# Routing logits of a fused two-layer block: routing weights as the stationary operand, in four column blocks, with one transpose back per group

## The chip, the cores and the metric

The kernel runs on one core of a Trainium2 chip. The metric is device time in microseconds (us) of one execution; the time before is the median of three runs. Engines are named as the profile does: PE is TensorE's matmul side and PEld its weight loads, DVE is VectorE, ACT is ScalarE, POOL is GpSimd, SP is SyncE.

## The reference

Two layers, each a gated attention-like step and a gated feed-forward step, on 32 sequences of 128 tokens with 128 features. All parts run in the kernel; the change touches the last one.

```python
x = x + tanh(g_xattn[0]) * L0_xattn(layernorm(x), ctx, ctx, ...)   # mLSTM, 8 heads
x = x + tanh(g_ffn[0])   * L0_ffn(layernorm(x), W1, b1, W2, b2)    # quantized, 128 -> 512 -> 128
x = x + tanh(g_xattn[1]) * L1_xattn(ctx, layernorm(x))             # dynamic time warping, then a gather-add
x = x + tanh(g_ffn[1])   * L1_ffn(layernorm(x), gate_weight, w1, b1, w2, b2)

def L1_ffn(x, gate_weight, w1, b1, w2, b2):
    logits = einsum('bld,ed->ble', x, gate_weight)          # 8 experts
    kth_val = sort(logits.reshape(-1))[4 * 128 * 6 - 1]     # over all sequences
    gates = logits * (logits >= kth_val)
    h = gelu(einsum('bld,ehd->bleh', x, w1) + b1)           # 128 -> 512
    y = einsum('bleh,edh->blde', h, w2) + b2.T              # 512 -> 128
    return einsum('blde,ble->bld', y, gates)
```

The routing logits are the product of the normed tokens with an 8 x 128 matrix. One threshold over all 32 x 128 x 8 logits decides which of them weigh an expert's output and which count as zero.

## The kernel before, in words

**Stages.** X, the residual, stays in SBUF with tokens on partitions: [128 tokens, 32 sequences, 128 features]. Four sequences make a group, so there are eight groups. The first layer runs up to about 229 us of the profiled execution. Then the warp (the second layer's alignment) is done twice by `warp_steps`, first for groups 0 to 2, alone on VectorE, then for groups 3 to 7. A row of it is a minimum (line 1058) and a scan (line 1059) on VectorE; `meet` (line 1003) and the turn-round at the end (lines 1098 and 1109) are small products. While the first warp runs, `second_dense` (lines 1241 to 1289) does the rest of the first layer's feed-forward on ScalarE, PE and GpSimd (line 1251 is GpSimd's add), and writes distances to DRAM (line 1236; for the first groups line 1156).

**The expert loop** starts at about 370 us. It has 64 units, one for a group and an expert. A unit has four products of 128 x 512 into `mph` (line 1494), each followed by a GELU on ScalarE into `hT` (line 1499), and sixteen products of 128 x 128 into `mpo` (line 1507). All are float32, and an fp32 product shows as two records on PE. The first 24 units are those of groups 0 to 2. Of the first 34 units (HELD) the output is copied (line 1515) and sent to DRAM, since its weight GA isn't known yet; from unit 34 on `combine` (lines 1457 and 1462) adds outputs to X on VectorE, the held ones read back among them. The program asks for GA there.

**The background.** Beside the units runs a generator, `background()`: `aligned(1)`, `aligned(2)`, the second warp, `aligned(3)` to `aligned(7)`, then `search()`. `pump(0.85)` after each mph, and after each four mpo, draws steps from it until the planned times that they yield add up. So a yield's number moves all later steps against the units. `aligned(0)` comes before the loop. Tile's scheduler then fixes the order of instructions on each engine at build time, and every engine keeps to its own order.

**One group's `aligned(g)`** (lines 1316 to 1364): masks `ge` and `pt` on VectorE (lines 1325 and 1327) and four products into `px` (line 1328) gather the aligned context; the residual add (line 1332) and the norm follow on VectorE, ending in `y` (line 1348); four transposes (line 1351) and a ScalarE copy give YT (line 1353), features on partitions. Then the routing logits: four products (line 1357), each with one sequence's 128 x 128 block of YT as the stationary operand and the routing weights `gws` (8 columns) as the moving one, give tokens on partitions and 8 columns for a sequence. VectorE copies these 32 columns into `lg` (line 1360).

**The search** (lines 1376 to 1401) finds the threshold bit by bit in 31 steps: VectorE counts (line 1371), PE sums over partitions (line 1373), VectorE decides (lines 1393 and 1394). It needs `lg` of all groups.

The PSUM pool `p_k` has a single buffer with the tag `small`, which the logits, the warp's small products and the search's sums share. In the first stage lines 453 and 614 write products with 32 stationary columns into blocks of 32 PSUM partitions; line 215 is the transposes of the first norm.

Of the kernel before, what the change touches and what calls it, by code (L numbers as in the profile page):

```python
# [8 lines left out]
F32 = mybir.dt.float32  # L9
# [9 lines left out]
P = 128  # L19
# [7 lines left out]
E = 8  # L27
KTH = 4 * 128 * 6
GB = 4
NG = B // GB  # L30
HW = 32
# [12 lines left out]
def tile_flamingo_gated(  # L44
# [21 lines left out]
    nc = tc.nc  # L66

    def pool(stack, name, bufs=1, space=None, side=None):
        kw = {} if space is None else {"space": space}
        kw.update({} if side is None else {"side": side})  # L70
        return stack.enter_context(tc.tile_pool(name=name, bufs=bufs, **kw))

    def new(p, shape, dt, tag, bufs=None):
        kw = {} if bufs is None else {"bufs": bufs}
        return p.tile(shape, dt, tag=tag, name=tag, **kw)
# [19 lines left out]
    gws = new(keep, [P, E], F32, "gws")  # L95
# [26 lines left out]
    ident = new(keep, [P, P], F32, "ident")  # L122
# [27 lines left out]
    def row_norm_steps(p, v, n, mean, r):  # L150

        m, w = (8, "") if n <= 8 else (16, "_w")
        bn = new(p, [P, m, 6], F32, "bn" + w)[:, 0:n]
        for i in range(n):
            nc.vector.bn_stats(bn[:, i, :], v[:, i, :])
            if i % 2 == 1:
                yield

        df = new(p, [P, m], F32, "bn_df" + w)[:, 0:n]
        nc.vector.tensor_tensor(df, bn[:, :, 1], bn[:, :, 4], ALU.subtract)  # L160
        ve = new(p, [P, m], F32, "bn_ve" + w)[:, 0:n]
        nc.vector.scalar_tensor_tensor(
            ve, bn[:, :, 2], D * 1e-5, bn[:, :, 5], ALU.add, ALU.add
        )
        nc.vector.scalar_tensor_tensor(mean, df, -0.5, bn[:, :, 1], ALU.mult, ALU.add)
        yield
        nc.vector.scalar_tensor_tensor(df, df, 0.25, df, ALU.mult, ALU.mult)
        nc.vector.scalar_tensor_tensor(ve, ve, 1.0 / D, df, ALU.mult, ALU.add)
        yield
        for _ in root_steps(p, ve, n, r):  # L170
            yield
# [116 lines left out]
    YT = new(wide, [P, B, S], F32, "YT")  # L288
    xst = new(wide, [P, 2, NG], F32, "xst")
    with ExitStack() as st:  # L290
        ap = pool(st, "attn")
        gp = pool(st, "gates")
        lp = pool(st, "ln", bufs=2)
# [105 lines left out]
        for k in range(6):  # L399
# [3 lines left out]
                rhs=one_c[0:1, :], start=True, stop=True,  # L403
# [6 lines left out]
        for k in range(2):  # L410
            hr_ps = new(p_at, [P, 4, S], F32, "at")
            nc.tensor.matmul(
                hr_ps, lhsT=sel.rearrange("p j c h -> p (j c h)"),
                rhs=ind[:, 4 * k : 4 * k + 4, :], start=True, stop=True,
# [303 lines left out]
        for p in range(B // 2 + 1):  # L718
# [4 lines left out]
            for u in range(3):  # L723
# [6 lines left out]
                g = p // 2 + 1  # L730
# [67 lines left out]
    with ExitStack() as st:  # L798
# [18 lines left out]
        with ExitStack() as st2:  # L817
# [26 lines left out]
            for n in range(4):  # L844
                for c in range(NC):
                    ph = new(p_h, [P, 2, 512], F32, "ph")
                    for k in range(2):
# [3 lines left out]
                            start=True, stop=True,  # L851
# [91 lines left out]
    def idle(busy, tie, value, n):  # L943

        if value is not None:
            rows = value.shape[0]
            one = onesb if value.dtype == BF16 else ones
            tie = nc.tensor.matmul(
                busy[:, 0 : value.shape[1]], lhsT=one[0:rows, :], rhs=value, start=True, stop=True
            )  # L950
        for _ in range(n):
            with tc.issue_after(getattr(tie, "ins", tie)):
                tie = nc.tensor.matmul(busy, lhsT=onesb, rhs=w1q, start=True, stop=True)  # L953
# [164 lines left out]
    with ExitStack() as st:  # L1118
        dp = pool(st, "dist", bufs=2)
        lp = pool(st, "lnA", bufs=2)  # L1120
# [16 lines left out]
        for g, ym2, ysq in normed:  # L1137
            d2 = new(dps, [P, GB, S], F32, "d2")
            nc.tensor.matmul(d2, lhsT=ones, rhs=ysq, start=True, stop=False)  # L1139
            for i in range(GB):  # L1140
                nc.tensor.matmul(
                    d2[:, i, :], lhsT=CD[:, GB * g + i, :], rhs=ym2[:, i, :],
                    start=False, stop=(i == GB - 1),
                )
            dd = new(dp, [P, GB, S], F32, "dd")
            for i in range(GB):
                b = GB * g + i
# [152 lines left out]
    with ExitStack() as st:  # L1300
        mp = pool(st, "moe")
        lp = pool(st, "last", bufs=2)
# [4 lines left out]
        p_k = pool(st, "p_k", space=PSUM)  # L1307
# [4 lines left out]
        lg = new(mp, [P, B * E], F32, "lg")  # L1312
        z = new(mp, [P, B * E], F32, "z")
        junk = new(mp, [P, B * E], BF16, "junk")

        def aligned(g):

            grp = slice(GB * g, GB * g + GB)
            xb = X[:, grp, :]
            px = new(p_x, [P, GB, D], F32, "px")  # L1320
            for i in range(GB):
                b = GB * g + i
                way = ends[0][:, :, b : b + 1] if b < BP else ends[1][:, :, b - BP : b - BP + 1]
                ge = new(lp, [P, S], BF16, "ge")
                nc.vector.tensor_scalar(ge, jota, way[:, 0], None, ALU.is_ge)
                pt = new(lp, [P, S], F32, "pt", bufs=4)
                nc.vector.scalar_tensor_tensor(pt, jota, way[:, 1], ge, ALU.is_le, ALU.mult)
                got = nc.tensor.matmul(  # L1328
                    px[:, i, :], lhsT=pt, rhs=CT[:, b, :], start=True, stop=True
                )  # L1330
                yield 0.65
            nc.vector.scalar_tensor_tensor(xb, px, tgx[:, 1:2], xb, ALU.mult, ALU.add)
            if g == 0:

                busy = new(p_k, [P, HID], F32, "small")
                idle(busy, got, None, 2)
                idle(busy, None, xb[:, 0, 0:4], 3)
            yield 0.8
            mean = new(lp, [P, 8], F32, "bn_mean")[:, 0:GB]
            r = new(lp, [P, 8], F32, "bn_r")[:, 0:GB]  # L1340
            for _ in row_norm_steps(lp, xb, GB, mean, r):
                yield 0.5
            if g == 0:
                idle(busy, None, mean, 6)
            tp = new(p_x, [P, GB, S], F32, "px")
            for i in range(GB):
                y = new(lp, [P, D], F32, "y", bufs=4)
                got = nc.vector.tensor_scalar(
                    y, xb[:, i, :], mean[:, i : i + 1], r[:, i : i + 1], ALU.subtract, ALU.mult
                )  # L1350
                nc.tensor.transpose(tp[:, i, :], y, ident)  # L1351
            held["normed"] = getattr(got, "ins", got)
            nc.scalar.copy(YT[:, grp, :], tp)
            yield 1.2
            lg_ps = new(p_k, [P, GB, E], F32, "small")
            for i in range(GB):
                nc.tensor.matmul(  # L1357
                    lg_ps[:, i, :], lhsT=YT[:, GB * g + i, :], rhs=gws, start=True, stop=True
                )
            got = nc.vector.tensor_copy(  # L1360
                lg[:, E * GB * g : E * GB * (g + 1)], lg_ps.rearrange("p b e -> p (b e)")
            )
            held["aligned", g] = getattr(got, "ins", got)
            yield 0.2
# [38 lines left out]
        def second_part():  # L1403

            with ExitStack() as st2:
                wp = pool(st2, "warpB", bufs=2, side="right")
                w1p = pool(st2, "warpB1", side="right")
                DV = CD[0 : 2 * (B - BP)].rearrange("p b s -> p (b s)").bitcast(BF16).rearrange(
                    "p (r s) -> p r s", s=S
                )  # L1410
                for w in warp_steps(
                    BP, B - BP, wp, w1p, lambda shape, tag: new(p_k, shape, F32, "small"),
                    nc.sync, DV, ends[1], masks[1],
                ):
                    yield w
            for g in range(NP, NG):
                for w in aligned(g):
                    yield w
            for w in search():
                yield w  # L1420

        def background():
            for g in range(1, NP):
                for w in aligned(g):
                    yield w
            for w in second_part():
                yield w
# [50 lines left out]
        for _ in aligned(0):  # L1478
            pass
# [6 lines left out]
        for n, (k, p, g, j) in enumerate(units):  # L1486
            e = 2 * p + j
# [4 lines left out]
            for c in range(NC):  # L1492
                ph = new(p_h, [P, GB * S], F32, "mph")
                got = nc.tensor.matmul(  # L1494
                    ph, lhsT=w1e[:, j, c * P : (c + 1) * P], rhs=tok, start=True, stop=True
# [9 lines left out]
            for i in range(GB):  # L1505
                for c in range(NC):
                    got = nc.tensor.matmul(  # L1507
                        po[:, i, :], lhsT=hT[c][:, i * S : (i + 1) * S], rhs=w2e[:, j, c, :],
                        start=(c == 0), stop=(c == NC - 1),
# [56 lines left out]
```

## Time and profile before

| what | us |
|---|---|
| median of 3 runs (lowest, highest) | 856.73 (856.17, 858.97) |
| span of the profiled execution | 854.5 |
| PE busy in it | 690.8 |
| VectorE busy | 591.8 |
| ScalarE busy | 449.7 |
| GpSimd busy | 66.7 |
| first and last start of a logits' product (line 1357) | 369.2, 565.7 |
| first and last start of a sum of the search (line 1373) | 566.7, 616.0 |

The span goes from the first to the last instruction of one execution; a run's time also holds what lies around it, 856.73 - 854.5 = 2.2 us for the median. The profile has the busy time of each engine, groups of instructions by line, and their order in time. In a row of the time order stand the start, the length, the engine, the line, the operation, output and inputs, sizes, the number of records, and in brackets the idle time before it and what ended it. PE's records overlap, so the distance from one start to the next, and not a record's length, is what a product takes of PE's time.

### The profile page before, as it was taken

What the parts mean: (1) busy time and instruction counts of PE and PEld (TensorE: products, weight loads), DVE (VectorE), ACT (ScalarE), POOL (GpSimd) and SP (SyncE); (2) the same over time, 40 slices, a digit from 0 to 9 for tenths busy, and PEclk for the clock granted to TensorE, in tenths of its full rate; (3) what the DMA queues carried; (4) which work ended last, traced back from release to release, by engine and by line L of the source; (5) the groups of instructions that cost most, each with busy time, mean ns of one, the idle gap of its engine ahead of it and who ended that gap; (6) DMA issues with size and microseconds to landing.
All of it is one profiled execution on the core that took longest, in us unless ns stands there. A gap on an engine that the chain in (4) does not pass through costs nothing.

```text
span 854.5 us, 13313 instructions
## 1 busy us (share of the span) xinstructions
PE 690.8 (81%) x4721; PEld 459.1 (54%) x4721; DVE 591.8 (69%) x2052; ACT 449.7 (53%) x791; POOL 66.7 (8%) x132
## 2 busy tenths in 40 slices
PE   5798998344242435589999999999999999999997
PEld 2244454211231223257777777766777777777776
DVE  7757999879858998889993666656705544444444
ACT  3787877496258888334444443443443433434332
POOL 2000000000401221100101010010010000000000
PEclk9897999555565555699999999999999999999999
DMA  8100000200021221023543020020013112121110
GB/s 326 38 2 13 2 3 2 80 20 0 0 42 36 55 61 32 13 60 98 157 138 100 38 87 25 38 74 32 31 63 87 50 37 87 38 65 56 52 51 26
DMA packets 20201, 47.32 MB, mean 55 GB/s; under 512 B 4014, under 2 KB 6942, under 8 KB 20110
## 3 DMA queue, kind: packets, MB, share of 16 engines
q1 hardware_dynamic: 14372, 29.69, 11.4%
q0 software_dynamic: 5056, 16.62, 6.2%
q8 instruction: 37, 0.61, 0.3%
q10 hardware_dynamic: 706, 0.16, 0.1%
q14 instruction: 30, 0.25, 0.1%
HBM read 27.12 MB, written 13.37 MB: 47 GB/s over the span
## 4 chain that ended last, share of the span: by engine, by line
PE 55%; DVE 20%; issue 2%; DMA 1%; ACT 1%; POOL 0%; SPq 0%; DVEq 0%; ACTq 0%
PE mph L1494 25%; PE mpo L1507 25%; DVE ru L1059 4%; DVE ru L1058 3%; DVE hit L1087 2%; DVE hst L858 2%; DVE hst L859 2%; PE px L1328 1%; PE small L1357 1%; PE px L1351 1%; DVE junk L1371 1%; PE po L916 1%; DMA d_dram<-dist 1%; PE busy L953 0%; PE d L1139 0%
## 5 line engine op out<-in xcount | busy, mean ns | idle before, releaser
L1507 PEld LDWEIGHTS mpo<-mw,hT 128*128 128x128 f32 x2048 | 249.7, 192 | 58.9 <-issue 39.7
L1499 ACT ACTIVATE hT<-mph,mb1s 128x512 f32<-128x512 f32 x256 | 175.6, 687 | 181.9 <-PE mph L1494 168.4
L1507 PE MATMUL mpo<-mw,hT 128*128 128x128 f32 x2048 | 256.3, 276 | 0.1
L1494 PE MATMUL mph<-YT,mw 128*128 128x512 f32 x512 | 244.1, 597 | 0.0
L1494 PEld LDWEIGHTS mph<-YT,mw 128*128 128x128 f32 x512 | 87.2, 192 | 57.9 <-issue 57.8
L1457 DVE TENSOR_TENSOR biased<-mpo,mb2s 128x512 f32<-128x512 f32 x28 | 19.4, 691 | 119.6 <-PE mpo L1507 119.6
L1462 DVE SCALAR_TENSOR_TENSOR X<-biased,GA,X 128x128 f32<-128x128 f32 x248 | 67.8, 344 | 0.1
L1515 ACT COPY ye<-mpo 128x512 f32<-128x512 f32 x34 | 19.9, 585 | 86.1 <-PE mpo L1507 83.5
L1059 DVE TENSOR_TENSOR_SCAN ru<-ru,dc 24x128 f32<-24x128 f32 (+1 forms) x128 | 54.0, 422 | 6.9 <-DMA dc<-d_dram 3.2
L1058 DVE TENSOR_TENSOR ru<-ru 24x128 f32<-24x128 f32 (+1 forms) x128 | 38.9, 304 | 3.2
L1516 POOL DMA_DIRECT2D y_dram<-ye x34 | 18.5, 543 | 224.9 <-ACT ye L1515 224.5
L562 ACT ACTIVATE dm<-bi 128x512 f32<-128x512 f32 x48 | 28.8, 603 | 7.9 <-PE bi L557 2.7
L604 DVE TENSOR_TENSOR sm<-sc,dm 128x512 f32<-128x512 f32 x32 | 21.7, 682 | 12.8 <-ACT dm L562 9.7
L1209 PE MATMUL po<-w2q,HT 128*128 128x128 bf16 x80 | 9.4, 311 | 25.5 <-ACT HT L1182 25.5
L849 PE MATMUL ph<-XQ,w1q 128*128 128x512 bf16 x32 | 15.8, 616 | 16.6 <-DVE XQ L840 9.2
L1276 PE MATMUL tp<-ident,y 128*128 128x128 f32 x20 | 8.1, 474 | 22.6 <-ACT y L1182 22.6
L1087 DVE SCALAR_TENSOR_TENSOR hit<-jotab,vw,YT 24x128 bf16<-24x128 bf16 x59 | 21.1, 357 | 4.1 <-DMA YT<-dv 2.0
L518 ACT ACTIVATE qm<-YT,mcol 128x512 f32<-128x512 f32 x32 | 23.1, 729 | 0.0
L1457 DVE TENSOR_TENSOR biased<-yl,mb2s 128x512 f32<-128x512 f32 x34 | 23.1, 680 | 0.0
L1209 PEld LDWEIGHTS <-HT 128*128 128x128 bf16 x80 | 8.1, 144 | 26.9 <-ACT HT L1182 26.9
L215 PE MATMUL at<-ident,y 128*128 128x128 f32 x32 | 8.1, 374 | 17.3 <-DVE y L211 16.9
L1087 DVE SCALAR_TENSOR_TENSOR hit<-jotab,vw,CD 40x128 bf16<-40x128 bf16 x59 | 20.3, 344 | 2.1
(389 smaller groups left out, 1021.0 us busy)
## 6 DMA issues: line engine op xcount, KB each, us to landing
y_dram<-ye POOLq DMA_DIRECT2D x34, 256.0 KB, 2.3
yl<-y_dram SPq DMA_DIRECT2D x34, 256.0 KB
mw<-in_mw POOLq DMA_DIRECT2D x12, 512.0 KB, 4.5
rblk<-ru SPq DMA_DIRECT2D x10, 288.8 KB
X<-in_x SPq DMA_DIRECT2D x4, 512.0 KB
CD<-in_ctx_d SPq DMA_DIRECT2D x4, 512.0 KB
CT<-in_ctx_t SPq DMA_DIRECT2D x4, 512.0 KB
mw<-in_mw SPq DMA_DIRECT2D x4, 512.0 KB
```

Source lines behind the costliest of these rows:

```text
L518: nc.scalar.activation(held["qm", g][:, h], YT[:, GB * g : GB * g + GB, :], AF.Copy, scale=mcol[:, h : h + 1],)
L562: done = nc.scalar.activation(dm, bi, AF.Exp)
L604: got = nc.vector.tensor_tensor(sm, scs[:, u], dm, ALU.mult)
L1058: nc.vector.tensor_tensor(u, ru[:, r, 0, 1 : S + 1], ru[:, r, 0, 0:S], ALU.min)
L1059: got = nc.vector.tensor_tensor_scan(ru[:, r + 1, 0, 1 : S + 1], u, dc[:, r, :], BIG, ALU.min, ALU.add)
L1087: nc.vector.scalar_tensor_tensor(hit, jotab[0:H2], vw[:, r + 1 : r + 2], near[:, r - r0, :] if r >= r0 else DV[:, r, :], ALU.is_le, ALU.mu ...
L1457: nc.vector.tensor_tensor(t, y, bias, ALU.add)
L1462: nc.vector.scalar_tensor_tensor(X[:, b, :], v[:, i, :], GA[:, E * b + e : E * b + e + 1], X[:, b, :], ALU.mult, ALU.add,)
L1494: got = nc.tensor.matmul(ph, lhsT=w1e[:, j, c * P : (c + 1) * P], rhs=tok, start=True, stop=True)
L1499: got = nc.scalar.activation(hT[c], ph, AF.Gelu_apprx_tanh, bias=mb1s[:, e, c : c + 1])
L1507: got = nc.tensor.matmul(po[:, i, :], lhsT=hT[c][:, i * S : (i + 1) * S], rhs=w2e[:, j, c, :], start=(c == 0), stop=(c == NC - 1),)
L1515: nc.scalar.copy(ye, po)
```

## The change

The routing weights become the stationary operand. `gwide` holds them in 32 columns, 8 of them filled and 24 zero; GpSimd makes it once. For each sequence of a group one product with `gwide` as weights and that sequence's 128 x 128 block of YT as the moving operand writes 32 partitions of one PSUM tile, so that four sequences fill its 128 partitions, experts on partitions and tokens in columns. ScalarE copies that tile to `lt`, the background yields 0.5, PE transposes `lt` back (once per group), and VectorE copies 8 of each 32 columns into `lg`.

```diff
@@ -1312,6 +1312,9 @@
         junk = new(mp, [P, B * E], BF16, "junk")
+        gwide = new(mp, [P, HW], F32, "gwide")
+        nc.gpsimd.memset(gwide[:, E:], 0.0)
+        nc.gpsimd.tensor_copy(gwide[:, 0:E], gws)
@@ -1352,13 +1355,20 @@
             yield 1.2
-            lg_ps = new(p_k, [P, GB, E], F32, "small")
+            lt_ps = new(p_k, [P, P], F32, "small")
             for i in range(GB):
                 nc.tensor.matmul(
-                    lg_ps[:, i, :], lhsT=YT[:, GB * g + i, :], rhs=gws, start=True, stop=True
-                )
+                    lt_ps[HW * i : HW * i + HW, :], lhsT=gwide, rhs=YT[:, GB * g + i, :],
+                    start=True, stop=True,
+                )
+            lt = new(lp, [P, P], F32, "lt")
+            nc.scalar.copy(lt, lt_ps)
+            yield 0.5
+            lg_ps = new(p_k, [P, GB, HW], F32, "small")
+            nc.tensor.transpose(lg_ps.rearrange("p b e -> p (b e)"), lt, ident)
             got = nc.vector.tensor_copy(
-                lg[:, E * GB * g : E * GB * (g + 1)], lg_ps.rearrange("p b e -> p (b e)")
+                lg[:, E * GB * g : E * GB * (g + 1)].rearrange("p (b e) -> p b e", e=E),
+                lg_ps[:, :, 0:E],
             )
```

## The prediction, made before the changed kernel ran

> **What bounds the kernel now.** I read the page first (its head, then the chain that ended last), then the busy times by stretch from the start of the expert loop, then the rows of the lines that the change touches, then PE in order of time. In the stretch rows the columns are the window, its length, the busy us and instruction count of PE, PEld, DVE, ACT and POOL, and the granted TensorE clock.
>
> ```profile
> span 854.5 us, 13313 instructions
> PE 690.8 (81%) x4721; PEld 459.1 (54%) x4721; DVE 591.8 (69%) x2052; ACT 449.7 (53%) x791; POOL 66.7 (8%) x132
> ```
>
> ```profile
> 376.00:500.00 124.00, 122.06 (x712) 89.66 (x711) 98.84 (x353) 55.78 (x84) 10.88 (x20) 1.00 0.30 98
> 500.00:566.00 66.00, 65.97 (x396) 48.69 (x395) 39.82 (x190) 28.89 (x44) 6.50 (x12) 1.00 0.20 64
> 566.00:617.00 51.00, 50.10 (x289) 34.25 (x289) 34.85 (x163) 20.69 (x31) 3.24 (x6) 1.00 0.08 32
> 617.00:854.50 237.50, 232.87 (x1338) 169.84 (x1336) 109.04 (x326) 92.12 (x135) 4.30 (x8) 1.00 0.19 55
> ```
>
> Over the whole span no engine is full; from 376 us to the end PE is, busy 471.0 of 478.5 us at full clock (1.00), and the chain that ended last runs along its expert products (mph 25%, mpo 25% of the span). So a microsecond of PE time, taken or added in any of the eight routing groups, is a microsecond of the end, unless a stall swallows it. The groups stand at 369.2 to 565.7 us, all but the first inside this stretch.
>
> ```profile
> L1357 PE MATMUL small<-gws,YT x64: 173/256/277, 369.2 to 565.7; 128*128 128x8 f32 x64
> ```
>
> ```profile
> 384.56 1.02 PE L1494 MATMUL mph<-YT,mw 128*128 128x512 f32 x2
> 385.42 0.95 PE L1357 MATMUL small<-gws,YT 128*128 128x8 f32 x8
> 386.23 0.47 PE L1328 MATMUL px<-CT,pt 128*128 128x128 f32 x2
> ```
>
> Each fp32 product is two records. The time rows are PE around group 1: start, length, work. Eight records of only 8 columns start at 385.42 and the next work at 386.23; inside, the starts are 0.112 us apart. The mpo records, 128 columns wide, also start 0.112 apart: what an 8-column product costs is its 128x128 weight load (192 ns, two in flight). **Removed per group: 8 x 0.112 = 0.89 us.**
>
> **What the new product costs.** Lines 453 and 215 in the first stage already do what the change does: 32-column weights into column blocks, between full-width transposes.
>
> ```profile
> 16.34 0.66 PE L215 MATMUL sc<-ident,y 128*128 128x128 f32 x4
> 16.92 1.06 PE L453 MATMUL at<-CD,W 128*32 128x512 f32 x6
> ...
> 24.47 1.92 PE L453 MATMUL at<-CD,W 128*32 128x512 f32 x16
> ...
> 41.94 1.91 PE L453 MATMUL at<-YT,W 128*32 128x512 f32 x8
> ...
> 44.37 1.91 PE L453 MATMUL at<-YT,W 128*32 128x512 f32 x4
> ```
>
> Sixteen, eight and four records take the same 1.91 us: four, two and one block, side by side, four turns of 0.43 us each. In single records, blocks of one turn start 7 ns apart. The batch at 16.92 prices the switch: from the last transpose to it 0.202 us, where transposes are 0.110 apart (+0.092); first to second turn 0.453 against 0.430 (+0.023); from its last start to the next transpose 0.523 against 0.430 (+0.093); that transpose waits for its weights, 0.165 against 0.110 (+0.055; an L1328 record that had to load took +0.08).
>
> So for four products of 128 columns: two turns of 0.110, plus 0.092 + 0.023 + 0.02 (stagger) + 0.093 + 0.08 = 0.53 us. The transpose back is one record: back to back at 41.35 us they are 0.110 apart. **Added per group: 0.53 + 0.11 = 0.64 us; net 0.64 - 0.89 = -0.25 us.** In group 0 PE waits 0.9 us for the YT copy anyway, so the 0.09 of its first switch is hidden. Eight groups: -8 x 0.25 - 0.09 = -2.1 us. Bounds: -2.6 (no exposed load, switches half hidden) to +3 (blocks one after another, see rivals).
>
> [...]
>
> **The added wait.** The transpose waits for ScalarE's copy of the four blocks, and in PE's queue the expert products stand behind it. From the first block's start: last record ends at 0.13 + 0.02 + 0.27 = 0.42 (a 64-column one of line 614 takes 219 ns, a 512-column one 592); hand-over 0.04; copy of 128 columns 0.27 (512 take 585, 256 take 378, line 633); hand-over 0.05: ready at 0.79. PE is through its blocks and the switch at 0.44, so 0.35 us of other PE work must lie between. In the built program's order there is, for groups 0 to 7: one mph (0.86), two px and one mpo (0.67), two mpo (0.45), four mpo (0.89), mph, mph, four mpo, mph. A GELU (687 ns) ahead of the copy in ScalarE's queue, as in groups 1 and 5, makes it ready at about 1.12, where PE arrives at 1.11 and 1.30. I take 0.1 us for all; bounds 0 and 4 (a GELU in the way every time). The copies themselves, 8 x 0.27 us, lie in ScalarE's idle time (28.89 busy of 66 us).
>
> **What the order moves.** The added yield of 0.5 shifts later steps of the background against the products.
> - PE waits for VectorE's y (line 1348) 1.1 us before group 1's transposes and 1.2 us before group 2's; VectorE has one gap (0.18 us) from 376 to 396 us, so its queue sets both. In the new order one step of the second warp's scan (line 1059, with line 1058 about 0.4 us) stands ahead of group 1's residual add (line 1332), where VectorE now waits 1.3 us for px; and the logits' copy (line 1360) comes late enough not to wait for PE (that gap). Both sets of transposes can then start some 0.7 us earlier, and before group 2's two more mpo (0.45 us) stand ahead, inside a wait that remains: 1.15 us, of which 0.6 is PE's own gain in groups 0 and 1, counted above. Of the other 0.55 I take -0.4 us; bounds 0 and -0.8.
> - In the threshold search (31 steps; line 1373) PE waits 0.22 to 0.28 us wherever the PE work between two counts is about 1.1 us, and nearly nothing where it is over 1.3: 12 waits, 2.9 us. The new order has 13 such short gaps: +0.2 us; bounds 0 and +0.5. The search ends in the order after 128 mph instead of 125, at unit 32; GA is needed at unit 34, 14 us later: nothing.
> - GpSimd's memset and copy of gwide stand ahead of line 1251's add, and wait for the same distance DMAs (line 1156) that it waited for; GpSimd then idles till 263.75 us for ScalarE. Cost nothing; were the cover gone, about 0.5 us. VectorE's copy keeps its 32 columns.
> - SyncE's queue stands as before, and so do all engines up to 368 us apart from gwide. PE's rows for the second warp's meeting point (line 1003) and end (line 1098) come a few products later; PE doesn't wait there, VectorE waited for PE 18.7 and 4.2 us and stays ahead of need.
>
> **Sum:** -2.1 + 0.1 - 0.4 + 0.2 = -2.2 us. The profiled span of 854.5 becomes 852.3. The median of the runs, 856.73, lies 2.2 us above the span, for start and end around it; so 854.5 us. A measurement of this kernel can tell about 0.3% from no change, which is 2.6 us: the forecast lies just inside that.
>
> **Rivals.**
> - *More than own time.* If the wait before group 2 shrinks by 0.8 and the switches are half hidden, -2.6 - 0.8 + 0.1 + 0.2 = -3.1: 853.6 us, faster. For it: PE waits on YT's copy near several groups, where a drain costs nothing. Against: those waits are under 0.15 us in groups 3 to 7.
> - *The transposes stall.* If a GELU stands before every copy, the copy is ready at 0.42 + 0.04 + 0.69 + 0.27 + 0.05 = 1.47; PE arrives at 0.89 to 1.33 and loses 0.15 to 0.6, say 0.35 on average: +2.8, total about 0.5 above before, 857.2: no change. Against: ScalarE's order has a GELU between YT's copy and the new one in two groups only.
> - *The blocks run one after another at 128 columns.* Then eight turns of 0.110 instead of two: 0.64 + 0.66 = 1.30 per group, 0.41 more than now; eight give +3.3, less 0.1 for waits and order (and 0.1 for group 0): 859.8 us, slower. The sign turns where the turns of a group take 0.5 us, between four and five of them; slower by over 0.3% needs nearly all eight alone. For it: the evidence has 512 and 64 columns, never 128, and group 0 has waits between its products. Against: line 614's 64-column records keep the same 7 ns.
> - *It doesn't do what it says.* The order could have torn the four products apart; it hasn't, they are adjacent in all eight groups.
>
> **How the numbers follow.** Own time with few stalls, spans from -1.0 to -3.4: 0.77, of which 0.40 beyond -2.6 and 0.37 within. Stalls on the copy: 0.11 (0.09 within, 0.02 slower). Blocks in series: 0.05, slower. Some other order effect in VectorE's queue, over 2.6 us: 0.07, 0.05 slower and 0.02 faster. So faster 0.42, same 0.46, slower 0.12. Of the likeliest case alone the range is 853.3 to 855.8; to hold 8 in 10 it goes down to 853.0 (-3.7, all bounds on the good side) and up to 857.6, past the stall case's 857.2.
>
> **What would show it.** The new logits' records should start in fours 7 ns apart, two turns 0.13 apart, and the next product 0.20 after the last; one transpose record per group, about 0.11 to 0.17 to its successor; PE's idle time named after the lt copy under 0.5 us in total; group 2's wait for y under 1.2 us; the search still about 51 us. If turns are four times as many, or the lt copy ends more than 1 us of PE idle time, or the span hasn't dropped by at least 1 us, the sum is wrong.

## The result: slower by 0.6%, against a forecast of a quarter per cent faster

| kernel | runs | median us (lowest, highest) |
|---|---|---|
| before | 18 | 857.14 (855.34, 864.90) |
| changed | 18 | 862.68 (859.99, 870.69) |

The ratio is 1.0061, 95% interval 1.0037 to 1.0086, about 5.2 us. The forecast was 854.5 us, with 853.0 to 857.6 as its range.

The page of the changed kernel, span and busy times, then the stretches that answer to those shown of before, 14 us later; the last ends with the span.

```profile
span 868.7 us, 13343 instructions
PE 699.8 (81%) x4729; PEld 459.3 (53%) x4729; DVE 592.1 (68%) x2052; ACT 452.3 (52%) x799; POOL 67.1 (8%) x134
```

```profile
390.00:514.00 124.00, 121.13 (x697) 87.57 (x696) 95.81 (x336) 56.30 (x86) 10.95 (x20) 0.99 0.31 98
514.00:580.00 66.00, 66.00 (x412) 47.86 (x411) 40.08 (x198) 29.09 (x48) 6.50 (x12) 1.00 0.20 64
580.00:631.00 51.00, 50.17 (x295) 33.88 (x294) 32.69 (x153) 21.44 (x33) 3.25 (x6) 1.00 0.09 33
631.00:868.70 237.70, 233.06 (x1338) 169.67 (x1337) 112.99 (x344) 92.34 (x135) 4.30 (x8) 1.00 0.19 55
```

The long stretches look as before. This span is 14.2 us longer than that of before, which is more than the medians differ, because 8.6 us of it arise in the first stage of this one execution: between 66 and 96 us the granted clock was 0.54 where before's profile has 0.83, and the first-stage instructions are the same. Experiment 3 below, which has the instructions of before, shows the same (0.60 from 66 to 100 us), and experiment 1, which has those of the change, doesn't (0.90 there), so it is no effect of the change. I therefore compare the **rest of each span, from the copy of `ends` (line 1112, VectorE) to its end**. That copy is the last step ahead of the stage that the change touches. Before, it stands at 359.74 us of 854.5: rest 494.76 us.

The new wait is found in VectorE's order of time, at the head of that stage (line 1328 of the changed kernel is line 1325 of before; all lines below are 3 to 10 further down). First before, then the changed kernel:

```profile
359.74 0.18 DVE L1112 COPY ends<-ends_ps 128x24 f32<-128x24 f32 x1 [1.28 <-PE ends_ps L1109]
360.05 0.48 DVE L1325 TENSOR_SCALAR ge<-jota,ends 128x128 bf16<-128x128 f32 x2
```

```profile
368.35 0.18 DVE L1112 COPY ends<-ends_ps 128x24 f32<-128x24 f32 x1 [1.28 <-PE ends_ps L1109]
375.23 0.48 DVE L1328 TENSOR_SCALAR ge<-jota,ends 128x128 bf16<-128x128 f32 x2 [6.70 <-DMA d_dram<-b]
```

`ge` of group 0 follows `ends` at once before, and after it stands still for 6.70 us until the DMA that writes `b`, a tile of the distance stage, to DRAM has landed. `ge` neither reads nor writes `b`. In the changed kernel's waits, the masks and then PE stand behind it, and GpSimd's issue of that DMA had itself waited for ScalarE:

```profile
POOL d_dram L1236 <- ACT b L1182: 13.3, 1, 13.3
ACT a L1182 <- PE d L1220: 8.5, 1, 8.5
...
PE px L1331 <- DVE pt L1330: 6.9, 1, 6.9
DVE ge L1328 <- DMA d_dram<-b: 6.7, 1, 6.7
```

The rest of the span is 868.7 - 368.35 = 500.35 us, 5.6 more than before: the size that the medians show. The theory formed from these rows: **memory, not instructions.** `lt` (two buffers of 512 bytes a partition) was put into the SBUF pool `last`, and `gwide` (128 bytes) into a pool below it. In the built program `last` lay below the memory of the distance stage's tiles `a` and `b`, with 512 bytes to spare; with the 1152 bytes it reaches over the first 640 of `a`'s 2048. The first tile of the pool, `ge`, then waits for everything that still uses `a` or `b`, the DMAs that read `b` included, though `ge` itself lies clear of both. The rival: the new products, their copy or the moved order cost the time.

### The profile page after: what moved, and what is told of

Read it like the earlier page. It is cut to its first block, busy times and chain, and to the rows that moved or that the text cites. A ratio compares the mean times of both kernels' runs of the same rounds, so it can differ in the third digit from the quotient of the medians.

```text
span 868.7 us, 13343 instructions
## 1 busy us (share of the span) xinstructions
PE 699.8 (81%) x4729; PEld 459.3 (53%) x4729; DVE 592.1 (68%) x2052; ACT 452.3 (52%) x799; POOL 67.1 (8%) x134
## 4 chain that ended last, share of the span: by engine, by line
PE 53%; DVE 10%; ACT 10%; issue 3%; DMA 2%; POOL 1%; DVEq 0%; ACTq 0%; POOLq 0%
PE mph L1504 24%; PE mpo L1517 24%; ACT HT L1182 4%; ACT y L1182 3%; DVE hst L858 2%; DVE hst L859 2%; DMA d_dram<-b 1%; DVE ru L1059 1%; PE px L1331 1%; DVE junk L1381 1%; PE po L916 1%; PE px L1354 1%; ACT b L1182 1%; ACT a L1182 0%; PE small L953 0%
## 5 line engine op out<-in xcount | busy, mean ns | idle before, releaser
L538 PE MATMUL sc<-qm,CD 64*128 64x256 f32 x128 | 22.9, 471 | 0.6 <-ACT YT L379 0.6
```

The costliest lines, as they stand in the source:

```text
L538: nc.tensor.matmul(scs[:, k, 4 * v : 4 * v + 4], lhsT=CD[kr, n, :], rhs=qm[kr, :, n % GB, SH:S], start=True, stop=True,)
```

## The experiments

In each the expectation was written before the run. "Rest" is the span less the start of the copy of `ends`, from one profile; before has 494.76.

**1. `lt` in another pool.** The changed kernel with `lt` in the pool `kth`, above `last`:

```diff
-            lt = new(lp, [P, P], F32, "lt")
+            lt = new(kp, [P, P], F32, "lt")
```

> The changed kernel with lt taken from the pool kth, which is opened after the pool last, instead of from last. Memory theory: last no longer reaches the memory of the first layer's distance tiles, so the first mask ge starts within 0.5 us of ends instead of after 6.7 us of idle time for the last distances' DMA; the time drops by 6 to 7 us against the changed kernel, to about 856 us, 0.997 to 1.001 of before. The order theory (the loss sits in the expert loop: VectorE's scan vv ahead of group 2's y, and the search) keeps 861 to 863 us, 1.005 or more of before.

```profile
359.30 0.18 DVE L1112 COPY ends<-ends_ps 128x24 f32<-128x24 f32 x1 [1.28 <-PE ends_ps L1109]
359.62 0.48 DVE L1328 TENSOR_SCALAR ge<-jota,ends 128x128 bf16<-128x128 f32 x2
```

Measured: the wait is gone. Median 854.95 us, ratio 0.9971 (0.9944 to 0.9998); span 852.6, rest 493.30, 1.5 less than before. So with `lt` elsewhere the changed kernel is a little faster than before (the interval ends just under 1), and what made it slower is where `lt` lies.

**2 and 3. The memory alone.** The kernel before, its products untouched, with its `y` tiles in `last` made wider by 40 or by 32 columns that nothing uses (four buffers: 640 or 512 bytes):

```diff
-                y = new(lp, [P, D], F32, "y", bufs=4)
+                y = new(lp, [P, D + 40], F32, "y", bufs=4)[:, 0:D]   # third kernel: D + 32
```

> The kernel before, its instructions and their order unchanged, with 640 bytes a partition more in the pool last (each y tile is 160 elements wide and its first 128 are used). Memory theory: last then ends 128 bytes inside the next pool, the first ge idles 6 to 7 us, and the time is 863 to 864 us, 1.007 to 1.009 of before. Order theory: as before, 857 us.

> The same with 512 bytes more: last ends exactly where the next pool begins. Memory theory: no overlap, no wait, as before, 857 us (0.998 to 1.002). If it is size as such or another place in memory that costs, it should lie near the kernel with 640 bytes.

With 640 bytes, then with 512, VectorE in order of time:

```profile
360.03 0.18 DVE L1112 COPY ends<-ends_ps 128x24 f32<-128x24 f32 x1 [1.28 <-PE ends_ps L1109]
366.91 0.48 DVE L1325 TENSOR_SCALAR ge<-jota,ends 128x128 bf16<-128x128 f32 x2 [6.69 <-DMA d_dram<-b]
```

```profile
368.47 0.18 DVE L1112 COPY ends<-ends_ps 128x24 f32<-128x24 f32 x1 [1.28 <-PE ends_ps L1109]
368.79 0.48 DVE L1325 TENSOR_SCALAR ge<-jota,ends 128x128 bf16<-128x128 f32 x2
```

Measured: 640 bytes give the same wait and 864.89 us (863 to 864 was expected), ratio 1.0079 (1.0043 to 1.0116), span 861.9, rest 501.87 (+7.1). 512 bytes give no wait: 859.58 us, ratio 1.0014 (0.9987 to 1.0041), span 863.4, rest 494.93 (+0.2). Empty bytes alone make the loss, and 128 of them decide it.

**4. The copy on VectorE.** In the changed kernel, and in experiment 1, PE stands still before group 2's transposes for longer than before. These are VectorE and PE of the changed kernel:

```profile
410.20 1.76 DVE L982 TENSOR_TENSOR_SCAN vv<-lf,to 80x774 bf16<-80x774 bf16 x1
411.88 1.08 DVE L1351 TENSOR_SCALAR y<-X,bn_mean,bn_r 128x128 f32<-128x128 f32 x4
```

```profile
412.25 0.33 PE L1354 MATMUL px<-ident,y 128*128 128x128 f32 x1 [2.03 <-DVE y L1351]
```

A scan step of the second warp's setting up, 1.76 us long, has moved ahead of `y` in VectorE's queue. In before it stands behind `y`, and PE's wait was 1.02 us:

```profile
396.66 1.11 DVE L1348 TENSOR_SCALAR y<-X,bn_mean,bn_r 128x128 f32<-128x128 f32 x4
397.69 1.76 DVE L982 TENSOR_TENSOR_SCAN vv<-lf,to 80x774 bf16<-80x774 bf16 x1
```

```profile
397.14 0.30 PE L1351 MATMUL px<-ident,y 128*128 128x128 f32 x1 [1.02 <-DVE y L1348]
```

The 1.2 and 2.2 us in the prediction and the expectations are the same two waits, counted from start to start. Experiment 1 with the copy on VectorE puts `y` first again:

```diff
-            nc.scalar.copy(lt, lt_ps)
+            nc.vector.tensor_copy(lt, lt_ps)
```

> lt from kth, and copied by VectorE instead of ScalarE. In the built order group 2's y then stands ahead of the scan vv (1.76 us) again, as before the change. Order theory for the rest: against the variant with ScalarE's copy the wait before group 2's transposes falls from 2.2 to about 1.2 us, and with it a half-clock window, 1.5 to 3 us in all: 853 to 855 us, 0.995 to 0.998 of before. Rival: VectorE's copies (8 of about 0.25 us) delay the second warp and the search and eat that; 856 us or more.

```profile
403.02 1.10 DVE L1351 TENSOR_SCALAR y<-X,bn_mean,bn_r 128x128 f32<-128x128 f32 x4
404.04 1.76 DVE L982 TENSOR_TENSOR_SCAN vv<-lf,to 80x774 bf16<-80x774 bf16 x1
```

Measured: PE's wait is 0.87 us. Median 855.13 us, ratio 0.9957 (0.9938 to 0.9977); span 859.7, copy of `ends` at 368.36, rest 491.34, 3.4 less than before and 2.0 less than experiment 1. Two things were changed here, the engine and the order, so:

**5. The order alone.** The copy stays on ScalarE; the yield ahead of the products is 0.5:

```diff
             nc.scalar.copy(YT[:, grp, :], tp)
-            yield 1.2
+            yield 0.5
```

> lt in the same pool as in the first of these kernels, its copy on ScalarE as in the change; the one edit beside that is the yield between YT's copy and the four blocks, 0.5 instead of 1.2, which puts group 2's y (line 1351) ahead of the scan step (line 982, 1.76 us) in VectorE's queue again. If the place of y in that queue is what the second yield cost, PE's wait before group 2's transposes is 1.0 to 1.2 us instead of 2.2, the stretch from the start of the expert stage to the end 3.0 to 3.6 us shorter than in the kernel before (with y behind the scan step it was 1.4 shorter), and the median 854 to 855.5 us. If instead the copy's engine made the difference between the two kernels with lt in that pool (VectorE against ScalarE), the wait stays at 2.2 us and the stretch at 1.2 to 1.6 shorter.

```profile
399.26 1.11 DVE L1351 TENSOR_SCALAR y<-X,bn_mean,bn_r 128x128 f32<-128x128 f32 x4
...
401.83 1.75 DVE L982 TENSOR_TENSOR_SCAN vv<-lf,to 80x774 bf16<-80x774 bf16 x1
```

```profile
399.65 0.33 PE L1354 MATMUL px<-ident,y 128*128 128x128 f32 x1 [1.18 <-DVE y L1351]
```

Measured: `y` is first, PE's wait 1.18 us. Median 855.02, ratio 0.9965 (0.9943 to 0.9986); span 857.1, copy of `ends` at 366.05, rest 491.05 (-3.7). It is the order that counts, not the copy's engine (the yield moves other steps too, so `y` is not quite alone in this). The medians of experiments 1, 4 and 5 lie within 0.2 us and their intervals overlap: the 2 us between them show in the profiles only.

**6. The products twice.** Experiment 1 with the four block products of a group issued two times into the same place.

```diff
-            for i in range(GB):
+            for i in [*range(GB), *range(GB)]:
                 nc.tensor.matmul(
                     lt_ps[HW * i : HW * i + HW, :], lhsT=gwide, rhs=YT[:, GB * g + i, :],
```

> lt in the other pool, and the four block products of each group issued twice, into the same place: eight instructions a group instead of four, with the same result. If the blocks run side by side and the switch is paid once a group, a group's block records last two turns of 0.114 us more, 0.58 us from first start to next work instead of 0.356, and eight groups +1.8 us on the end: median 856 to 858 us, the spread of the clock included. If blocks of 128 columns ran one after another, +0.9 us a group, +7 in all. If each change of block had its own switch, +0.4 to +0.7 us a group, +3 to +6 in all. The place of y against the scan step in VectorE's queue is as with single products (behind it).

PE around group 3, first single (experiment 1), then doubled:

```profile
521.82 0.43 PE L1360 MATMUL small<-YT,gwide 128*32 128x128 f32 x8
522.18 1.16 PE L1517 MATMUL mpo<-mw,hT 128*128 128x128 f32 x8
```

```profile
526.17 0.64 PE L1360 MATMUL small<-YT,gwide 128*32 128x128 f32 x16
526.75 1.16 PE L1517 MATMUL mpo<-mw,hT 128*128 128x128 f32 x8
```

Measured: from a group's first start to the next work 0.58 us against 0.36, in every group that ran at full clock (all but group 2). Four more products cost 0.22 us, two turns: blocks run side by side, and the switch is paid once. Median 859.23, ratio 1.0015 (0.9992 to 1.0038); the median is above the 856 to 858 that I named. The profile carries the sum better: span 858.1, copy of `ends` at 362.92, rest 495.18, 1.9 more than experiment 1 against the 1.8 expected.

**7 and 8. 128 bytes in the changed kernel itself.** Seventh: `lt` has one buffer and stays in `last`. Eighth: `gwide` is moved to `kth` as well, so that `last` ends where `a` begins.

```diff
-            lt = new(lp, [P, P], F32, "lt")
+            lt = new(lp, [P, P], F32, "lt", bufs=1)              # seventh and eighth
-        gwide = new(mp, [P, HW], F32, "gwide")
+        gwide = new(kp, [P, HW], F32, "gwide", bufs=1)           # eighth alone
```

> The changed kernel with one buffer for lt instead of two; lt stays in the pool last. The pool now ends 640 bytes a partition further up than in the kernel before (lt 512, and 128 of gwide below it), 128 bytes above where the distance stage's a begins. If any overlap with that memory holds up the pool's first tile, ge of group 0 (line 1328) still waits 6.7 us for the DMA d_dram<-b, and the median is 861 to 865 us, as with two buffers. If the wait grew with the overlapped bytes, or needed an overlap with b itself, it is gone: 854 to 857 us. One buffer alone delays nothing: a group's lt is read 40 us before the next copy, or in the last five groups 10 us.

> As the one before, and gwide in the pool kth instead of moe: the pool last now ends exactly where a begins, and every instruction of PE, VectorE, ScalarE and SyncE stands in the order of the changed kernel; GpSimd's two for gwide stand behind its DMAs of b. Lt is still in the pool last. If the overlap is the cause, these 128 bytes decide: ge follows the copy of ends within 0.2 us as before, and the stretch from there to the end is about 1.4 us shorter than in the kernel before (y of group 2 is behind the scan step still, PE waits 2.2 us there); median 854.5 to 856.5 us. Risk: gwide now waits for those DMAs, to about 366.5 us, before the first use at 368.8. If the wait comes from something else in the change, the median stays at 861 to 865 us.

```profile
361.35 0.18 DVE L1112 COPY ends<-ends_ps 128x24 f32<-128x24 f32 x1 [1.28 <-PE ends_ps L1109]
368.18 0.48 DVE L1328 TENSOR_SCALAR ge<-jota,ends 128x128 bf16<-128x128 f32 x2 [6.64 <-DMA d_dram<-b]
```

```profile
362.81 0.18 DVE L1112 COPY ends<-ends_ps 128x24 f32<-128x24 f32 x1 [1.28 <-PE ends_ps L1109]
363.13 0.48 DVE L1328 TENSOR_SCALAR ge<-jota,ends 128x128 bf16<-128x128 f32 x2
```

Measured: seventh 863.52 us, ratio 1.0075 (1.0048 to 1.0102), rest 861.8 - 361.35 = 500.45 (+5.7), as in the changed kernel; eighth 854.85 us, ratio 0.9972 (0.9944 to 1.0001), rest 856.3 - 362.81 = 493.49 (-1.3). The two kernels have the same order on PE, VectorE, ScalarE and SyncE. An overlap of 128 bytes with `a` costs as much as the changed kernel's 640. The overlap lies in `a` and the DMA waited for reads `b`, so the wait goes by the old pool and not by the tile overlapped; that is shown for this pair of pools alone. The risk named for the eighth didn't come in: `gwide` was filled at 369.75 us, the first product that reads it started at 372.31.

## Why the prediction was wrong, step by step

Three points on PE divide the rest: the starts of the 1st, 16th and 32nd record of the expert products mph. Each entry is the length of that part less its length before, from the start times of the two profiles; the end is that of the last instruction. The entries are rounded one by one, and the sums can differ by 0.1 from those above, which use the page's rounded span.

| part of the rest | changed, us | experiment 1, us |
|---|---|---|
| copy of `ends` to the 1st mph (group 0) | +6.6 | -0.5 |
| to the 16th mph (up to group 1's transposes) | -1.6 | -1.4 |
| to the 32nd mph (group 1's products, group 2) | +2.3 | +2.3 |
| to the end (groups 3 to 7, search) | -1.7 | -1.7 |
| sum | +5.6 | -1.4 |

- **The step that failed** is the fourth point of "What the order moves": "all engines up to 368 us" stand as before "apart from gwide", with gwide priced at nothing. The order of instructions did stand; a wait in it did not. I costed gwide's two instructions and lt's copy, but not the bytes that they take. The wait is worth 6.7 us in its own row and 7.1 us to the end (experiment 2); behind it PE resumes at half clock, 0.50 from 375.2 to 382.2 us in the changed kernel, which may be the 0.4 between the two. None of my rivals had it. The one on the slower side, blocks one after another, fell: a group's blocks are 7 ns apart and take 0.36 us.
- **The new product's own cost held.** Forecast 0.53 us for the blocks and 0.11 for the transpose. Measured in groups 3 to 7 of experiment 1: entry 0.205 where 0.112 is the usual step (+0.093), 0.356 from first start to next work, the next load exposed by 0.10, transpose 0.109: 0.66 against 0.64. A transpose's record is 272 ns long, which is not what PE pays (rows of the changed kernel, where the next record starts 0.109 us after it in six of the eight groups, 0.110 and 0.116 in the others):

```profile
L1360 PE MATMUL small<-YT,gwide x64: 272/297/423, 385.0 to 584.2; 128*32 128x128 f32 x64
```

```profile
L1368 PE MATMUL small<-ident,lt x8: 272/272/280, 386.3 to 585.4; 128*128 128x128 f32 x8
```

- **The removed products were sized a little small.** Forecast 0.89 us a group. In before's groups 3 to 7 it is 0.86 to 0.89 us from their first start to the next work, and the load of that next work is exposed by 0.08, which the forecast left out: 0.94 to 0.97.
- **The added wait held too**: the lt copy takes 257 to 272 ns (forecast 0.27), and PE has other products until it is there. In the changed kernel 400.08 to 400.30 us is an mpo, and the transpose follows without a gap.
- **VectorE's order was mis-signed.** Forecast -0.4, with "two more mpo" inside "a wait that remains". I counted one scan step (lines 1058 and 1059) ahead of group 1's residual add, and overlooked the 1.76 us of line 982 that moved ahead of group 2's `y`. PE's wait grew from 1.02 to 2.03 us. The rest of the +2.3 is the clock: PE's row at 0.50 for 3.4 us from 413.2 us in the changed kernel. The seventh kernel has the wait without that row, and +0.8, so the slow row is worth about 1.5. Experiments 4 and 5, with `y` first, have neither.
- **The -1.4 to -1.6 before group 1 was not forecast as such.** The half-clock stretch that before has from 371.0 to 374.4 us (0.50), after its first group, is absent there; experiments 2 and 3, with the products of before, have it too (0.50 for 3.4 us from 378.1 and 379.3 us), and experiments 1, 4, 5 and 6 don't (1.00). It is present (0.50 from 379.1 to 382.5 us), and the gain is missing, in the seventh kernel (0.0), which in turn has none in group 2 (+0.8 instead of +2.3).
- **The search**: first to last sum 49.4 us against 49.3; +0.2 was forecast. The last row of the table is -1.7, where the sum has 5 x -0.25 + 0.2 = -1.1. The removed products, at about 0.95 instead of 0.89, account for about half of the difference: 5 x (0.66 - 0.95) + 0.1 = -1.35. The other 0.35 is open.

With the wait away and `y` first (experiments 4 and 5) the rest falls by 3.4 and 3.7 us, of which some 1.5 are the half-clock stretch that is absent after group 0: what remains is near the -2.2 of the sum, though these are other kernels, in another order, than the one forecast. Both beat the kernel before, at 0.9957 and 0.9965; which of the two is better the runs can't say.

## What to carry to other kernels

A tile added to a pool changes addresses as well as work: before pricing the instructions, see which older tiles the pool's memory now overlaps, what last reads them, a DMA to DRAM above all, and how long after the pool's first use that ends. An unchanged order of instructions says nothing about their waits, so compare what each waits for as well. Where a background's steps shift, count every step that moves ahead of a needed one by its own duration: a single one of 1.76 us, with the slower clock behind it, cost 2.3 us, about what eight groups' saving of a quarter microsecond brings.

## What was unexpected of the hardware

- **The clock fell after one wait of PE of about 2.0 us and not after another.** After about 2.0 us of idle PE at 410 us the changed kernel ran at 0.50 from 413.2 to 416.6 us; this is PE's clock in the stretch rows, before, during and after:

```profile
410.00:413.20 3.20, 1.17 (x12) 0.97 (x11) 3.20 (x9) 0.00 (x0) 0.00 (x0) 1.00 0.32 98
413.20:416.60 3.40, 3.40 (x22) 2.79 (x21) 2.47 (x7) 0.85 (x2) 0.00 (x0) 0.50 0.10 38
416.60:420.00 3.40, 3.40 (x16) 1.97 (x15) 2.79 (x10) 2.38 (x4) 0.54 (x1) 1.00 0.20 77
```

  PE is full in the middle row and yet pays about 1.5 us, by the comparison with the seventh kernel above; in the row before it PE was busy for 1.17 of 3.20 us. Before has such a stretch (0.50) of 3.4 us at 371.0 us. The seventh kernel has the same wait of PE in group 2 and no such stretch after it.
  What the profiles show of the times: in those of before and of the changed kernel all half-clock stretches begin whole multiples of 3.413 us apart (before, among others: 251.5, 285.6, 371.0 and 852.2 us; the last three lie 34.1, 119.5 and 600.7 us behind the first, which is 10, 35 and 176 times 3.413). Cut into steps of that length, counted from such a start, the changed kernel and experiment 1 have group 2's wait within one step: PE is busy for 1.38 of its 3.41 us in the first and about 1.4 in the second, and the next step runs at 0.50. In the seventh kernel the same wait falls across two steps, busy for 1.83 and 2.97 us, and the clock stays at 1.00. That the place of the wait in the steps makes the difference is a reading of these three profiles, which no run tested. For group 0 the busy time settles nothing: 2.73 us in the step before before's stretch at 371.0 us, and 2.73 in the same place of experiment 5, which has no such stretch (1.00 from 366 to 402 us). What decides there is open.
- **The same first stage took up to 9 us more.** Over the profiles of this study the copy of `ends` stood anywhere from 359.30 to 368.47 us, with the same work ahead of it; in the two profiles compared above the clock between 66 and 96 us was 0.83 and 0.54. What sets it wasn't tried. Between two single profiles, a difference of 2 us can be read only from a stage behind it.
